# One sort of all 16,384 tokens ahead of the last feed-forward instead of four block sorts, with its rank table and three more row buffers

## The chip, the core and the metric

The kernel runs on one core of a Trainium2 chip. The core has five engines with a queue each, which work on their own and wait for each other by semaphores: TensorE (PE: matrix products and transposes into PSUM), VectorE (DVE), ScalarE (ACT), GpSimd (POOL) and SyncE (SP, which here only starts transfers). Transfers between HBM and the on-chip SBUF run on 16 DMA engines; the indirect ones, which take row numbers from a tile, are started by POOL. Tiles have 128 partitions (rows).

The metric is device time in microseconds (us) of one execution, from the first to the last instruction and what lies around it. Times are medians of several executions. A profile is one execution on its own.

## The reference

Two layers, each a graph convolution and a feed-forward part, over 64 batches of 256 tokens with 256 features. The change lies in the last step, the feed-forward of layer 1, and in how its tokens are ordered:

```python
x = x + _L0_gnn_ref(_layernorm(x), adj, ...)
x = x + _L0_ffn_ref(_layernorm(x), ...)          # a recurrent (LSTM) step over 256 tokens
x = x + _L1_gnn_ref(_layernorm(x), adj, ...)
x = x + _L1_ffn_ref(_layernorm(x), ...)

def _L1_ffn_ref(x, ...):                          # 16,384 tokens, 1024 units
    t = jnp.max(xx[:, None, :] + Wt[None, :, :], axis=-1) + bt
    cvx = jnp.max(z * sl_cvx + of_cvx, axis=-1)   # z = t, 8 lines per unit
    ccv = jnp.min(z * sl_ccv + of_ccv, axis=-1)
    trop = s * cvx + (1.0 - s) * ccv
    classical = gelu(xf @ Wc + bc)
    g = sigmoid(xf @ Wg + bg)
    return (g * trop + (1.0 - g) * classical) @ Wd + bd
```

The costly line is the first: for each token and each of 1024 units a maximum over 256 features of feature plus weight.

## The kernel before

**Stages.** The kernel is one program. The first 2647 us of the profile are the graph step of layer 0, the recurrent step, the preparation of the feed-forward's units, and the graph step of layer 1. That last one (`Batch`, one batch of 256 tokens at a time) also finds, for every token, how many of its 256 features can decide a maximum at all. This number goes to `need`, a tile with one column for each of the 128 groups of 128 tokens. It writes the token's normalised features and a copy with the undecided features masked to `pay_d`, and the residual to `res_d`, both in DRAM.

**Ranks.** The feed-forward (the pools `w4` and following, from L1227) never computes the maximum over 256 features. A token with `need` = 9 only needs its 9 largest features. For tokens with about the same need to share a tile of 128, the tokens are sorted by need, largest first. `RANKS` (L41) says how many features the tiles of a block get, in order: the first tile 40, the second 19, and so on down to 2. If more tokens need many features than the table has room for, a flag is raised (`late`, L243; `over`), and after everything else a dense computation replaces the result (from L1428).

**Blocks.** `RANKS` has 32 entries, so `NB` = 32 tiles (4096 tokens) are sorted together and there are `NSB` = 4 blocks. `sorted_block` (L1247) calls `sort` (L213) for a block and turns the result into row numbers, `perm`. Block 0 is sorted ahead of the loop (L1388); blocks 1 to 3 inside it, each two groups ahead of its first use (L1406).

**What `sort` does.** It is a counting sort on DVE and PE, with `bins` = 41 and `nb` tiles. It makes a one-hot array (bin, tile) of every partition (L221), sums it over the partitions with PE (L236), scans it (L238), adds the places of earlier partitions (L248 and L249), and reduces to a place for each token (L252). It then turns places into an order: `rhot`, a one-hot of the row within a tile (nb × 128 elements, L263), and `thot`, a one-hot of the tile (nb × nb elements, L270, L276, L282), whose nb products on PE (L285) give the token at each place.

**Groups and the loop.** Four tiles of a block make a group (`GT` = 4), chosen so that the ranks of a block's 8 groups come out nearly equal (`mixed`): 47, 36, 36, 35, 35, 35, 34 and 35. Thirty-two groups go through a pipeline (L1392). Iteration g does, four times (once for each tile q):

- `down` of group g−2 (PE, L1218), added to the residual on DVE (L1225), and `give_back`: POOL scatters the result to the output (L1374);
- `ask` of group g+1: POOL gathers 128 token rows from `pay_d` (L1285); `pick`: DVE takes the largest features eight at a time (L1297 to L1300: value, index, removal), PE transposes the features and ACT copies them (L1306);
- `maxplus` of group g: for every rank POOL gathers one row of the weights for each token into a row buffer (L1314, 128 rows of 4 KB), and DVE folds it into `acc` with one instruction (L1323); the first rank of a tile is done by ACT (L1320);
- `classical` of group g−1 (PE, L1338; ACT, L1345) and `fuse`: PE transposes `acc` (L1355), ACT and DVE evaluate the lines (L1200 to L1210, ending in `fu`);
- `ask_rest` of group g−1: POOL gathers the residual rows (L1363).

The row buffers are the pool `row4` with 10 tiles: POOL can start a gather only when the tenth row before it has been used. All gathers and scatters stand in POOL's one queue, in a fixed order.

**What orders the work.** The order on each engine is settled when the program is built: the framework lists every engine's instructions in an order of its own making, near to that of the code, and adds the semaphores. At run time each engine takes its instructions strictly in that order.

Of the kernel before, what the change touches and what calls it, by code (L numbers as in the profile page):

```python
# [11 lines left out]
BF16 = mybir.dt.bfloat16  # L12
# [25 lines left out]
SHIFT = 40.0  # L38
LOW = 2.1
REST = 0.1  # L40
RANKS = [40, 19, 16, 15, 14, 13, 12, 12, 11, 11, 10, 10, 9, 9, 8, 8]  # L41
RANKS += [8, 7, 7, 6, 6, 6, 5, 5, 5, 4, 4, 3, 3, 3, 2, 2]
NEG = -1e30


# [12 lines left out]
def kernel(ctx: ExitStack, tc: tile.TileContext, a: dict, out: bass.AP):  # L58
# [16 lines left out]
    nc = tc.nc  # L75
# [20 lines left out]
    rows = const.tile([P, K], F32, name="rows")  # L96
# [12 lines left out]
    need = const.tile([P, NT], F32, name="need")  # L109
# [13 lines left out]
    num_f = const.tile([P, P], F32, name="num_f")  # L123
# [9 lines left out]

    NB = len(RANKS)
    NSB = NT // NB
# [77 lines left out]
    def sort(sp, psum, need, room, over, tag):  # L213


        nb, bins = need.shape[1], room.shape[1]
        cnt = sp.tile([P, nb], F32, name=f"cnt_{tag}", tag="cnt")
        nc.vector.tensor_scalar(cnt, need, float(bins - 1), None, ALU.min)
        nc.vector.tensor_scalar(cnt, cnt, -1.0, float(bins - 1), ALU.mult, ALU.add)
        hot = sp.tile([P, bins, nb], BF16, name=f"hot_{tag}", tag="hot")  # L220
        nc.vector.tensor_tensor(  # L221
            hot,
            cnt.unsqueeze(1).to_broadcast([P, bins, nb]),
            num_f[:, :bins].unsqueeze(2).to_broadcast([P, bins, nb]),
            ALU.is_equal,
        )
# [11 lines left out]
        nc.vector.tensor_tensor_scan(  # L238
            pos_c, ones[:, 0:1].to_broadcast([P, bins * nb]), tot_c, 0.0, ALU.mult, ALU.add
        )  # L240
        nc.vector.tensor_tensor(pos, pos, tot, ALU.subtract)
# [10 lines left out]
        nc.vector.tensor_reduce(at, pos.rearrange("p k i -> p i k"), AX.X, ALU.add)  # L252
        at_i = sp.tile([P, nb], I32, name=f"ati_{tag}", tag="at_i")
        til = sp.tile([P, nb], F32, name=f"til_{tag}", tag="til")
        row = sp.tile([P, nb], F32, name=f"row_{tag}", tag="row")
        nc.vector.tensor_copy(at_i, at)
        nc.vector.tensor_scalar(at_i, at_i, P - 1, None, ALU.bitwise_and)
        nc.vector.tensor_copy(row, at_i)
        nc.vector.tensor_tensor(til, at, row, ALU.subtract)
        nc.vector.tensor_scalar(til, til, 1.0 / P, None, ALU.mult)  # L260

        rhot = sp.tile([P, nb, P], BF16, name=f"rhot_{tag}", tag="tot")
        nc.vector.tensor_tensor(  # L263
            rhot,
            row.unsqueeze(2).to_broadcast([P, nb, P]),
            num_f.unsqueeze(1).to_broadcast([P, nb, P]),
            ALU.is_equal,
        )
        thot = sp.tile([P, nb, 2, nb], BF16, name=f"thot_{tag}", tag="pos")
        nc.vector.tensor_tensor(  # L270
            thot[:, :, 0, :],
            til.unsqueeze(2).to_broadcast([P, nb, nb]),
            num_f[:, :nb].unsqueeze(1).to_broadcast([P, nb, nb]),
            ALU.is_equal,
        )
        nc.vector.tensor_tensor(  # L276
            thot[:, :, 1, :],
            thot[:, :, 0, :],
            num_f[:, :nb].unsqueeze(2).to_broadcast([P, nb, nb]),
            ALU.mult,  # L280
        )
        nc.vector.tensor_scalar(thot[:, :, 0, :], thot[:, :, 0, :], rows[:, 0:1], None, ALU.mult)  # L282
        pp = psum.tile([P, 2, nb], F32, name=f"pp_{tag}", tag="pc")
        for i in range(nb):
            nc.tensor.matmul(  # L285
                pp, rhot[:, i, :], thot[:, i, :, :], start=(i == 0), stop=(i == nb - 1)
            )
# [57 lines left out]
    with (  # L345
# [18 lines left out]
        class Batch0:  # L364


            def __init__(self, b):
                self.b = b
# [747 lines left out]
    class FeedForward:  # L1116


        def __init__(self, wp, pools, units_sorted):
            self.p4, self.u4, self.cgp, self.ps_c, self.ps_o = pools  # L1120
# [21 lines left out]
            self.s_b = wp.tile([P, NF], F32, name="s_b")  # L1142
            nc.scalar.activation(self.s_a, col["alpha"], AF.Sigmoid)
            nc.vector.tensor_scalar(self.s_b, self.s_a, -1.0, 1.0, ALU.mult, ALU.add)

        def classical(self, xr, tag):

# [76 lines left out]
                    )  # L1224
                nc.vector.tensor_tensor(res[c], res[c], po[:, c, :], ALU.add)  # L1225

    with (  # L1227
        tc.tile_pool(name="w4", bufs=1) as wp,
        tc.tile_pool(name="s4", bufs=1) as sp,
        tc.tile_pool(name="pay4", bufs=5) as payp,  # L1230
        tc.tile_pool(name="xr4", bufs=3) as xrp,
        tc.tile_pool(name="res4", bufs=7) as resp,
        tc.tile_pool(name="tk4", bufs=8) as tkp,
        tc.tile_pool(name="row4", bufs=10) as rowp,
        tc.tile_pool(name="acc4", bufs=8) as accp,
        tc.tile_pool(name="p4", bufs=2) as p4,
        tc.tile_pool(name="u4", bufs=3) as u4,
        tc.tile_pool(name="cg4", bufs=2) as cgp,
        tc.tile_pool(name="fu4", bufs=1) as fup,
        tc.tile_pool(name="ps_c4", bufs=6, space=PSUM) as ps_c,  # L1240
        tc.tile_pool(name="ps_o4", bufs=2, space=PSUM) as ps_o,
    ):
# [4 lines left out]
        def sorted_block(blk):  # L1247


            order = sort(  # L1250
                sp, ps_c, need[:, blk * NB : (blk + 1) * NB], room, over[:, blk : blk + 1], blk
            )
            nc.vector.tensor_copy(perm[blk][:, 0, :], order)
            nc.vector.tensor_scalar(order, order, float(blk * NB * P), None, ALU.add)
            nc.vector.tensor_copy(perm[blk][:, 1, :], order)

        ff = FeedForward(wp, (p4, u4, cgp, ps_c, ps_o), True)

        def place(i, of):
            j = i % NB  # L1260
# [124 lines left out]
            if 0 <= g < NGR:  # L1385
                getattr(groups[g], piece)(*args)

        sorted_block(0)  # L1388
        for q in range(GT):
            groups[0].ask(q)  # L1390
            groups[0].pick(q)
        for g in range(NGR + 2):  # L1392
            for q in range(GT):
                if q == 0:
                    for part in range(GT // NC):
                        each(g - 2, "down", part)
                    each(g - 1, "classical", 0)
                each(g + 1, "ask", q)
                each(g, "maxplus", q)
                each(g - 1, "fuse", q)  # L1400
                if q + 1 < GT:
                    each(g - 1, "classical", q + 1)
                each(g + 1, "pick", q)
                each(g - 1, "ask_rest", q)
                each(g - 2, "give_back", q)
            if g % GPB == GPB - 2 and g + 2 < NGR:  # L1406
                sorted_block((g + 2) // GPB)

# [19 lines left out]
    with tc.If(bad > 0):  # L1428
        with (
# [9 lines left out]
            ff = FeedForward(wp, (p4, u4, cgp, ps_c, ps_o), False)  # L1439
# [123 lines left out]
```

## Time and profile before

| | us |
|---|---|
| time, median of 3 (lowest, highest) | 5418.49 (5399.26, 5419.93) |
| the profiled execution: its time | 5431.3 |
| the profiled execution: its span | 5429.4 |
| sort of block 0 begins, ends | 2646.81, 2674.35 |
| first group's results reach L1225 | 2839.45 |
| last group's results reach L1225 | 5408.23 |

Row gathers (L1314) take 1453.8 us of POOL over 1172 instructions, a mean of 1240 ns; the folding on DVE (L1323) 1317.5 us over 1044, a mean of 1282 ns. The page's table of groups has them as the two costliest lines of the whole kernel.

How to read it: the page gives the busy time of each engine over the whole span, then 40 equal slices of it in tenths, the DMA queues, the chain that ended last, the costliest groups of instructions with the idle time before them and what ended it, and the DMA issues. Where a stage has its own limits, the same trace is asked for the busy time of each engine in a stretch of it, for the list of waits (who waited for whom), and for the instructions in order of time (the timeline; a number in brackets is the idle time before an instruction and what ended it). L1225 is line 1225 of the code before.

### The profile page before, as it was taken

How to read it: one execution, taken by the hardware profiler on the slowest of the kernel's cores; microseconds unless marked ns; L12 is line 12 of the kernel's file. 1: busy time of each engine (PE TensorE's matmuls, PEld its weight loads, DVE VectorE, ACT ScalarE, POOL GpSimd, SP SyncE). 2: the span in 40 equal slices, each digit the busy share in tenths (PEclk: the TensorE clock that was granted, in tenths of full speed). 3: DMA queues.
4: the chain of work that ended last, by engine and by line, in shares of the span. 5: the costliest groups of instructions: out<-in, count | busy, mean ns of one | idle time of the engine just before them, and what ended most of it. 6: DMA issues, size and time to landing. Idle time of an engine off the chain costs nothing. (4 is left out here: it accounts for less than half of the span.)

```text
span 5429.4 us, 58641 instructions
## 1 busy us (share of the span) xinstructions
PE 4221.3 (78%) x17791; PEld 2368.5 (44%) x17792; DVE 4189.6 (77%) x9226; ACT 2273.9 (42%) x4245; POOL 2588.7 (48%) x2739
## 2 busy tenths in 40 slices
PE   8999889999999968888457666677675776757777
PEld 5666533333333346666334443344343443434344
DVE  6777686555555568888788798888898889888897
ACT  3555411222222235555344544455444554445455
POOL 2333400000000035555487667777767777677774
PEclk9999999999999989999678878788787888878889
DMA  4222213111111134444487776877767787777774
GB/s 134 84 82 86 79 21 83 32 28 28 28 28 28 28 108 138 139 139 138 153 304 255 252 254 206 270 252 266 244 224 266 244 272 241 231 260 246 267 253 141
DMA packets 448128, 886.59 MB, mean 163 GB/s; under 512 B 54328, under 2 KB 279100, under 8 KB 447804
## 3 DMA queue, kind: packets, MB, share of 16 engines
q0 software_dynamic: 192448, 685.96, 37.7%
q1 hardware_dynamic: 253476, 193.64, 12.5%
q8 instruction: 143, 2.34, 0.2%
q10 hardware_dynamic: 1880, 3.16, 0.2%
q14 instruction: 181, 1.48, 0.1%
HBM read 773.32 MB, written 110.26 MB: 163 GB/s over the span
## 5 line engine op out<-in xcount | busy, mean ns | idle before, releaser
L1314 POOL DMA_INDIRECT row<-wT_d,num x1172 | 1453.8, 1240 | 547.3 <-issue 271.3
L1323 DVE SCALAR_TENSOR_TENSOR acc<-row,val,acc 128x1024 f32<-128x1024 f32 x1044 | 1317.5, 1282 | 178.2 <-DMA row<-wT_d,num 165.6
L1218 PE MATMUL po<-w_d,fu 128*128 128x256 f32 x2048 | 599.6, 439 | 102.4 <-DVE fu L1210 95.5
L1338 PE MATMUL pc_gg<-xr,w_gt 128*128 128x512 f32 x1024 | 539.9, 669 | 96.0 <-ACT u L1206 60.8
L575 PE MATMUL pg<-w_hh,hT 128*64 128x512 f32 x2040 | 501.5, 613 | 91.4 <-DVE hT L702 91.0
L956 POOL TENSOR_TENSOR adjT<-adjT,ident 128x128 f32<-128x128 f32 x128 | 57.7, 473 | 1020.2 <-DMA adjT<-in_adjT_dram 1012.6
L1218 PEld LDWEIGHTS po<-w_d,fu 128*128 128x128 f32 x2048 | 425.6, 219 | 270.0 <-DVE fu L1210 148.2
L1338 PE MATMUL pc_cl<-xr,w_c 128*128 128x512 f32 x1024 | 490.5, 620 | 20.9 <-issue 11.3
L1206 ACT ACTIVATE u<-pa,prm 128x512 f32<-128x512 f32 x512 | 383.4, 778 | 265.3 <-DVE v L1207 239.0
L575 PE MATMUL pg<-w_ih,XT 128*64 128x512 f32 x2048 | 488.1, 598 | 2.9 <-issue 2.9
L1320 ACT ACTIVATE acc<-row,val 128x1024 f32<-128x1024 f32 x128 | 146.9, 1147 | 762.0 <-DMA row<-wT_d,num 761.8
L682 ACT ACTIVATE sg<-pg 128x256 f32<-128x256 f32 x256 | 98.3, 384 | 839.5 <-PE pg L575 833.3
L1207 DVE SCALAR_TENSOR_TENSOR v<-u,prm,v 128x512 f32<-128x512 f32 x512 | 377.2, 750 | 36.8 <-ACT u L1206 36.0
L1355 PE MATMUL pa<-ident,acc 128*128 128x128 f32 x1024 | 196.6, 327 | 266.4 <-ACT u L1206 91.6
L1338 PEld LDWEIGHTS pc_gg<-xr,w_gt 128*128 128x128 f32 x1024 | 208.8, 213 | 357.7 <-issue 208.6
L173 DVE TENSOR_SCALAR xn<-x,mv,rstd 128x256 f32<-128x256 f32 x512 | 224.9, 454 | 136.5 <-POOL rstd L166 128.5
L1338 PEld LDWEIGHTS pc_cl<-xr,w_c 128*128 128x128 f32 x1024 | 199.6, 201 | 252.5 <-issue 226.7
L1355 PEld LDWEIGHTS pa<-ident,acc 128*128 128x128 f32 x1024 | 146.1, 168 | 341.1 <-ACT u L1206 102.9
L575 PEld LDWEIGHTS pg<-w_ih,XT 128*64 128x64 f32 x2048 | 149.3, 139 | 301.8 <-issue 301.8
L688 DVE TENSOR_TENSOR cc<-sg,cc 128x128 f32<-128x128 f32 x255 | 74.8, 293 | 261.9 <-ACT sg L682 260.6
L1305 PE MATMUL ptx<-ident,pay 128*128 128x128 f32 x256 | 65.6, 346 | 265.5 <-ACT u L1206 123.8
L1200 ACT ACTIVATE v<-pa,prm 128x512 f32<-128x512 f32 x256 | 199.0, 777 | 170.6 <-DVE fu L1210 149.4
(394 smaller groups left out, 8327.0 us busy)
## 6 DMA issues: line engine op xcount, KB each, us to landing
adjT<-in_adjT_dram SPq DMA_DIRECT2D x128, 256.0 KB, 3.3
row<-wT_d,num POOLq DMA_INDIRECT x1172
x<-in_x_dram SPq DMA_DIRECT2D x64, 256.0 KB, 2.7
x_d<-x SPq DMA_DIRECT2D x64, 256.0 KB, 2.5
x1s<-x_d SPq DMA_DIRECT2D x128, 128.0 KB, 2.9
x_d<-x1s SPq DMA_DIRECT2D x128, 128.0 KB, 2.5
x<-x_d SPq DMA_DIRECT2D x64, 256.0 KB, 2.8
res_d<-x SPq DMA_DIRECT2D x64, 256.0 KB, 3.8
```

Of the source, the lines that this page charges most:

```text
L173: nc.vector.tensor_scalar(xn[:, c, :], x[:, c, :], mv[:, c, 0:1], rstd[:, c : c + 1], ALU.subtract, ALU.mult)
L575: ins = nc.tensor.matmul(half(pg, j), by(k), gates_of(w, k, j), start=False, stop=(last and k == K - 1), tile_position=(0, j * B),)
L682: nc.scalar.activation(sg, pg[:, : 2 * P], AF.Sigmoid)
L1200: nc.scalar.activation(v, pa, AF.Identity, bias=prm[:, f, 1:2], scale=prm[:, f, 0:1])
L1206: nc.scalar.activation(u, pa, AF.Relu, bias=of, scale=sc)
L1207: nc.vector.scalar_tensor_tensor(v, u, sg, v, ALU.mult, ALU.add)
L1218: nc.tensor.matmul(po[:, c, :], fused(f, c), self.w_d[:, f, :], start=False, stop=(f == NF - 1),)
L1314: nc.gpsimd.indirect_dma_start(row, None, wT_d, bass.IndirectOffsetOnAxis(ap=self.num[q][:, r : r + 1], axis=0))
L1320: nc.scalar.activation(acc, row, AF.Identity, bias=v)
L1323: nc.vector.scalar_tensor_tensor(acc, row, v, acc, ALU.add, ALU.max)
L1338: nc.tensor.matmul(pc, wgt[:, k, f * P : (f + 1) * P], self.xr[:, k, :], start=(k == 0), stop=(k == K - 1),)
L1355: nc.tensor.transpose(pa[:, q * P : (q + 1) * P], self.acc[q][:, f * P : (f + 1) * P], ident)
```

## The change

The rank table has 128 entries instead of 32, so that the same code makes one block of 128 tiles: `NB` = 128, `NSB` = 1. Its entries sum to 1065; four times the old table is 1172. The groups become 32 of one block, with 43, 35, 35, 34, 33 and then 32 to 34 ranks. `pay_d`, `res_d` and `perm` become one tensor each. There is one call of `sort` with 5248 elements in its (bin, tile) arrays, and it stands ahead of the loop in pools of its own, which are closed before the loop's pools are opened. The two calls of `sorted_block` go. In `sort` the one-hots are made in chunks of 16 tiles with two alternating buffers, and the scaling of `thot` by the row number moves from DVE to ACT. The row buffers go from 10 to 13. `FeedForward` gets its pools by a method of its own (`use`), since it is now built before they are.

```diff
-RANKS = [40, 19, 16, 15, 14, 13, 12, 12, 11, 11, 10, 10, 9, 9, 8, 8]
-RANKS += [8, 7, 7, 6, 6, 6, 5, 5, 5, 4, 4, 3, 3, 3, 2, 2]
+RANK_COUNTS = (
+    (40, 1), (24, 1), (21, 1), (19, 1), (18, 1), (17, 2), (16, 3), (15, 3), (14, 4), (13, 5),
+    (12, 6), (11, 7), (10, 9), (9, 9), (8, 11), (7, 11), (6, 11), (5, 11), (4, 11), (3, 9), (2, 7),
+    (1, 4),
+)
+RANKS = [rank for rank, count in RANK_COUNTS for _ in range(count)]
...
-        rhot = sp.tile([P, nb, P], BF16, name=f"rhot_{tag}", tag="tot")
...
-        nc.vector.tensor_scalar(thot[:, :, 0, :], thot[:, :, 0, :], rows[:, 0:1], None, ALU.mult)
         pp = psum.tile([P, 2, nb], F32, name=f"pp_{tag}", tag="pc")
...
+        ch = min(nb, 16)
+        for i0 in range(0, nb, ch):
+            some = slice(i0, i0 + ch)
+            rhot = sp.tile([P, ch, P], BF16, name=f"rhot_{tag}_{i0}", tag=f"rhot{i0 // ch % 2}")
+            nc.vector.tensor_tensor(
+                rhot,
+                row[:, some].unsqueeze(2).to_broadcast([P, ch, P]),
+                num_f.unsqueeze(1).to_broadcast([P, ch, P]),
+                ALU.is_equal,
+            )
+            thot = sp.tile([P, ch, 2, nb], BF16, name=f"thot_{tag}_{i0}", tag=f"thot{i0 // ch % 2}")
+            nc.vector.tensor_tensor(thot[:, :, 0, :], ..., ALU.is_equal)
+            nc.vector.tensor_tensor(thot[:, :, 1, :], ..., ALU.mult)
+            nc.scalar.activation(thot[:, :, 0, :], thot[:, :, 0, :], AF.Copy, scale=rows[:, 0:1])
+            for i in range(ch):
+                nc.tensor.matmul(
+                    pp,
+                    rhot[:, i, :],
+                    thot[:, i, :, :],
+                    start=(i0 + i == 0),
+                    stop=(i0 + i == nb - 1),
+                )
...
-        tc.tile_pool(name="s4", bufs=1) as sp,
...
-        tc.tile_pool(name="row4", bufs=10) as rowp,
...
+        with (
+            tc.tile_pool(name="s4", bufs=1) as sp,
+            tc.tile_pool(name="ps_s4", bufs=2, space=PSUM) as ps_s,
+        ):
+            for blk in range(NSB):
+                order = sort(
+                    sp, ps_s, need[:, blk * NB : (blk + 1) * NB], room, over[:, blk : blk + 1], blk
+                )
+                nc.vector.tensor_copy(perm[blk][:, 0, :], order)
+                nc.vector.tensor_scalar(order, order, float(blk * NB * P), None, ALU.add)
+                nc.vector.tensor_copy(perm[blk][:, 1, :], order)
...
+        rowp = ctx4.enter_context(tc.tile_pool(name="row4", bufs=13))
...
-        sorted_block(0)
         for q in range(GT):
             groups[0].ask(q)
...
-            if g % GPB == GPB - 2 and g + 2 < NGR:
-                sorted_block((g + 2) // GPB)
```

More of the change, by code (lines that the diff above doesn't have):

```diff
@@ L260, in sort @@
         nc.vector.tensor_scalar(til, til, 1.0 / P, None, ALU.mult)
-        rhot = sp.tile([P, nb, P], BF16, name=f"rhot_{tag}", tag="tot")
[L263 to L281, printed above, removed]
-        nc.vector.tensor_scalar(thot[:, :, 0, :], thot[:, :, 0, :], rows[:, 0:1], None, ALU.mult)
-        pp = psum.tile([P, 2, nb], F32, name=f"pp_{tag}", tag="pc")
-        for i in range(nb):
-            nc.tensor.matmul(
-                pp, rhot[:, i, :], thot[:, i, :, :], start=(i == 0), stop=(i == nb - 1)
-            )
+        pp = psum.tile([P, 2, nb], F32, name=f"pp_{tag}", tag="pc")
@@ new lines, in sort @@
+        ch = min(nb, 16)
[7 more added lines that the diff above has]
+                ALU.is_equal,
+            )
+            thot = sp.tile([P, ch, 2, nb], BF16, name=f"thot_{tag}_{i0}", tag=f"thot{i0 // ch % 2}")
+            nc.vector.tensor_tensor(
+                thot[:, :, 0, :],
+                til[:, some].unsqueeze(2).to_broadcast([P, ch, nb]),
+                num_f[:, :nb].unsqueeze(1).to_broadcast([P, ch, nb]),
+                ALU.is_equal,
+            )
+            nc.vector.tensor_tensor(
+                thot[:, :, 1, :],
+                thot[:, :, 0, :],
+                num_f[:, some].unsqueeze(2).to_broadcast([P, ch, nb]),
+                ALU.mult,
+            )
[8 more added lines that the diff above has]
+                )
@@ L1116, with __init__ @@
     class FeedForward:
-        def __init__(self, wp, pools, units_sorted):
-            self.p4, self.u4, self.cgp, self.ps_c, self.ps_o = pools
+        def __init__(self, wp, units_sorted):
             self.w_c = wp.tile([P, K, FF], F32, name="w_c")
@@ L1144, in __init__, with use @@
             nc.vector.tensor_scalar(self.s_b, self.s_a, -1.0, 1.0, ALU.mult, ALU.add)
+        def use(self, p4, u4, cgp, ps_c, ps_o):
+            self.p4, self.u4, self.cgp, self.ps_c, self.ps_o = p4, u4, cgp, ps_c, ps_o
         def classical(self, xr, tag):
@@ L1225, in down @@
                 nc.vector.tensor_tensor(res[c], res[c], po[:, c, :], ALU.add)
-    with (
-        tc.tile_pool(name="w4", bufs=1) as wp,
-        tc.tile_pool(name="s4", bufs=1) as sp,
[L1230 to L1233, printed above, removed]
-        tc.tile_pool(name="row4", bufs=10) as rowp,
[L1235 to L1242, printed above, removed]
+    with ExitStack() as ctx4:
+        wp = ctx4.enter_context(tc.tile_pool(name="w4", bufs=1))
         room = room_of(wp, RANKS)
@@ L1245 @@
         over = wp.tile([P, NSB], F32, name="over")
[L1247 to L1257, printed above, removed]
+        ff = FeedForward(wp, True)
+        with (
[5 more added lines that the diff above has]
+                    sp, ps_s, need[:, blk * NB : (blk + 1) * NB], room, over[:, blk : blk + 1], blk
+                )
+                nc.vector.tensor_copy(perm[blk][:, 0, :], order)
+                nc.vector.tensor_scalar(order, order, float(blk * NB * P), None, ALU.add)
+                nc.vector.tensor_copy(perm[blk][:, 1, :], order)
+        payp = ctx4.enter_context(tc.tile_pool(name="pay4", bufs=5))
+        xrp = ctx4.enter_context(tc.tile_pool(name="xr4", bufs=3))
+        resp = ctx4.enter_context(tc.tile_pool(name="res4", bufs=7))
+        tkp = ctx4.enter_context(tc.tile_pool(name="tk4", bufs=8))
+        rowp = ctx4.enter_context(tc.tile_pool(name="row4", bufs=13))
+        accp = ctx4.enter_context(tc.tile_pool(name="acc4", bufs=8))
+        p4 = ctx4.enter_context(tc.tile_pool(name="p4", bufs=2))
+        u4 = ctx4.enter_context(tc.tile_pool(name="u4", bufs=3))
+        cgp = ctx4.enter_context(tc.tile_pool(name="cg4", bufs=2))
+        fup = ctx4.enter_context(tc.tile_pool(name="fu4", bufs=1))
+        ps_c = ctx4.enter_context(tc.tile_pool(name="ps_c4", bufs=6, space=PSUM))
+        ps_o = ctx4.enter_context(tc.tile_pool(name="ps_o4", bufs=2, space=PSUM))
+        ff.use(p4, u4, cgp, ps_c, ps_o)
         def place(i, of):
@@ L1438 @@
         ):
-            ff = FeedForward(wp, (p4, u4, cgp, ps_c, ps_o), False)
+            ff = FeedForward(wp, False)
+            ff.use(p4, u4, cgp, ps_c, ps_o)
             w_t = wp.tile([P, NF, D], F32, name="w_trop")
```

## The prediction

> **What bounds the kernel now.** First the page's busy shares and slices. The sort and the feed-forward are the last 2782 us of the span (from 2646.8), and VectorE (DVE) is the fullest engine there.
>
> ```profile
> PE 4221.3 (78%) x17791; PEld 2368.5 (44%) x17792; DVE 4189.6 (77%) x9226; ACT 2273.9 (42%) x4245; POOL 2588.7 (48%) x2739
> ...
> DVE  6777686555555568888788798888898889888897
> ```
>
> Then the busy time by stretch. Columns: stretch, its length, busy us (and instructions) of PE, weight loads, DVE, ACT, POOL, then granted clock, DMA share, GB/s.
>
> ```profile
> 2646.80:2674.70 27.90, 6.06 (x41) 3.69 (x42) 24.60 (x34) 0.00 (x0) 0.01 (x1) 0.50 0.23 85
> 2674.70:2839.45 164.75, 75.42 (x192) 35.84 (x192) 138.27 (x192) 59.78 (x79) 132.46 (x107) 0.68 0.87 300
> 3537.93:3619.14 81.21, 55.54 (x169) 30.81 (x170) 70.71 (x98) 41.57 (x56) 59.16 (x49) 0.86 0.73 245
> 3174.87:3245.50 70.63, 46.88 (x135) 27.34 (x136) 68.08 (x99) 28.37 (x40) 51.00 (x38) 0.77 0.70 228
> 3245.50:3358.57 113.07, 76.89 (x249) 42.74 (x248) 92.09 (x135) 45.40 (x64) 75.78 (x54) 0.79 0.61 202
> 3358.57:3455.75 97.18, 55.29 (x161) 31.77 (x160) 83.50 (x110) 42.29 (x55) 72.71 (x57) 0.72 0.83 273
> 2839.45:5375.64 2536.19, 1763.02 (x5385) 999.64 (x5386) 2188.09 (x3044) 1212.51 (x1624) 1827.72 (x1441) 0.83 0.75 249
> ```
>
> The first row is the first block's sort: DVE alone, the others wait. The second is the fill, before the first group comes out. From 2839.45 on I cut the time where DVE does the first L1225 of each group; 30 rounds up to 5375.64. Nineteen of them (the third row is one) average 82.7 us with about 70 of DVE. Three times in the run three rounds (rows four to six: 280.9 us; the other two triples 269.7 and 271.4) hold a block's sort and its 47-rank group; the last two rounds are short (69.9 and 72.1). Over the 30 rounds DVE idles 2536 − 2188 = 348 us. The waits of DVE and of POOL in that stretch name the causes:
>
> ```profile
> DVE acc L1323 <- DMA row<-wT_d,num: 147.9, 41, 10.3
> DVE res L1225 <- remote: 62.1, 14, 6.3
> ...
> POOL row L1314 <- ACT acc L1320: 150.7, 65, 5.2
> ```
>
> (us, times, longest.) DVE starves for gathered rows 148 us in all, and hands over to `down` some 8 us a round (6.1 + 1.1 + 0.8 in the timeline). POOL meanwhile waits 151 us for ACT, and 48 for DVE, to give a row buffer back. So DVE bounds the loop, with POOL just behind: a round issues some 47 indirect DMAs, and by the rows
>
> ```profile
> L1314 POOL DMA_INDIRECT row<-wT_d,num x1083 | 1341.6, 1239 | 520.2 <-issue 251.2 <-ACT acc L1320 150.7 <-DVE acc L1323 47.9
> L1323 DVE SCALAR_TENSOR_TENSOR acc<-row,val,acc 128x1024 f32<-128x1024 f32 x969 | 1221.5, 1282 | 157.8 <-DMA row<-wT_d,num 147.9 <-ACT xr L1306 5.6 <-PE ptx L1305 2.2
> ```
>
> that is 47 × (1.24 + 0.30 between two) = 72 us of POOL.
>
> **The sort, +88 us.** One sort of 128 tiles replaces the first one (2646.81 to 2674.35: 27.5 us). It stands where DVE alone works, so all of it is on the path; POOL's first asks wait for `perm`, and PE, ACT and the DMA queues wait for those. Rows of the first sort:
>
> ```profile
> 2651.25 2.89 DVE L238 TENSOR_TENSOR_SCAN pos<-ones,tot 128x1312 f32<-128x1312 f32 x1
> 2654.17 1.52 DVE L241 TENSOR_TENSOR pos<-pos,tot 128x1312 f32<-128x1312 f32 x1
> ...
> 2659.34 2.34 DVE L252 TENSOR_REDUCE at<-pos 128x32 f32<-128x1312 f32 x1
> ...
> 2663.78 4.42 DVE L263 TENSOR_TENSOR rhot<-row,num_f 128x4096 bf16<-128x4096 f32 x1
> ```
>
> 1312 elements take 1.52 us and 4096 take 4.42: 1.04 ns an element and 0.16 fixed. The (bin, tile) arrays grow to 41 × 128 = 5248 elements: three such ops (L221, L241, L250) 5.6 each, 16.8; the scan 11.1; the reduce 8.9; the eleven copies and eleven adds at the pitch of the first sort (0.60 for 512) 12.4. One-hots: eight chunks of three ops of 2048, 24 × 2.29 = 55. Some twenty small ops 4. Sum 108. The scaling goes to ACT: 128x1024 takes 1.15 and 128x512 0.69 there, so 2.1 for 2048; PE does 16 products a chunk. Both lie under the 6.9 us that DVE spends on the next chunk, save behind the last: 2.1 + 3.4 + 2 of hand-over. So 115.5, less 27.5: +88. If each chunk waited for ACT and PE (two chunk buffers), 8 × 5.5 more: +132; if nothing waited and the broadcasts ran like the cheapest row, +75.
>
> **Sorts and 47-rank groups inside the loop, −77 us.** The nine rounds of the triples take 822.0, nine plain ones 744.7. The three later sorts, and the 11 or 12 ranks by which those groups exceed the others, go. By busy time it is three times about 34 us (243.7 in the triple shown, against 3 × 70), so up to −102; at least −60 if the lull in the first round of each was itself a gain.
>
> **Ranks elsewhere, −85 us.** The tables sum to 4 × 293 = 1172 before and 1065 after. Leaving out the groups with 47 and the fill, 35.1 a round become 32.9: 2.24 × 30 = 67 ranks. Each is a gather on POOL (1.54) and an op on DVE, which follow at 1.2 us; I take DVE's 1.2, being the fullest: 81, and 4 for four groups with one pick round fewer (three ops of a third of a us). Ends: 0.76 × 1.2 (in the triples 34 us of DVE work cost 26) gives 61, POOL's 1.54 gives 103. The fill has five ranks fewer at the 1.6 us of its pace: −8.
>
> **13 row buffers, −70 us.** No row of before has three more buffers. The ends are −148, all of DVE's wait for rows, and +18: three more rows in the queue may hold up `pay`, for which L1297 waits 18.4 us now, as long again. In the programs as built, when POOL comes to a group's first write-out it has issued 10 rows more than DVE used by then, and 13 after; the numbers of rows between write-outs stay. In the round of 3537.93 DVE then runs dry for 6.6 us, behind POOL's 15 us of write-outs and reads of `res` and `pay`. Three more rows with what lies between them are about 4.5 us of DVE work. Cutting 4.2 off each plain round's idle time beyond 8 gives 2.9 a round, 87 in 30; I take 2.3, since POOL (45 DMAs, 70 us) has little slack.
>
> The smaller sort at 811 us only moves one 0.23 us op to ACT, inside the recurrent stage: nothing; uncovered, 1 us. The 41 fills of `room` and the weight loads stay ahead of the sort.
>
> **Sum.** +88 − 77 − 85 − 8 − 70 = −152. The profiled execution took 5431.3 (span 5429.4): 5279. It lies 12.8 above the median of three, 5418.5; on that base 5266.
>
> **Rivals.** *Buffers change nothing*, because the dry spell is POOL's stretch of small DMAs: 5266 + 70 = 5336. For it: DMA share falls to 0.2 to 0.4 in that stretch and is near 1.0 behind it. Against: the stock at its start is what grows.
>
> *POOL becomes the bound*, as its issues stretch beside a denser DVE: at the 1.5 us of many gathers, 45 × 1.80 = 81 us a round, loop 30 × 81 − 24 = 2406, so −130 + 88 − 8 = −50: 5368. Against it, POOL beside eight back-to-back L1323:
>
> ```profile
> 3605.11 0.94 POOL L1314 DMA_INDIRECT row<-wT_d,num  x1 [0.31 <-issue]
> 3606.36 0.94 POOL L1314 DMA_INDIRECT row<-wT_d,num  x1 [0.30 <-issue]
> ```
>
> The Trainium skill, "SBUF — State Buffer", section "Who interferes with whom", says that a VectorE op with two SBUF inputs contends with a GpSimd instruction that reads SBUF, one holding the other off; L1323 is such an op. By that rule this rival would hold; the trace agrees only in part, with 0.94 beside many of them.
>
> *Slower: the loop is not DVE's*, but the chain of hand-overs (DVE's last `fu`, PE's `down`, L1225; ACT's `u`, DVE's `v`). Then sorts and ranks come out of idle time, and only the sort's +88 and the fill's −8 stay: 5498. It decides once the 206 us of DVE work taken out (three sorts of 22, 107 ranks of 1.2, 12 of picks) give back under 80. For it: 8 us of hand-over in each round. Against: 70 of 82.7 us busy, and extra work in the triples that cost three quarters of itself.
>
> *It doesn't do what it says*: more tokens need many ranks than the new table has, a bin is late (L243), and the dense path at the end runs: 8 × 256 × 8 DVE ops of 128x2048, 2.35 us each by the rows of 512 and 1024, 38 ms. Counted from the reference's inputs, each count of the table holds with at least 99 tokens to spare.
>
> **How the numbers follow.** As summed, 5215 to 5315: 0.58. Buffers change nothing: 0.17. POOL's bound: 0.10. Better than 5215 (POOL's price for ranks, all row waits gone): 0.08. Slower: 0.06. Dense path: 0.01. The range 5195 to 5365 leaves out the last two and half of the two ahead of them, 0.16. About 0.5%, 27 us, is what a measurement can tell: faster 0.91, same 0.03, slower 0.06.
>
> **What would show it.** Sort: about 115 us of DVE alone ahead of the first ask. Rounds: no more triples, 76 to 78 us each with DVE about 67 busy; 937 L1323 ops. Buffers: DVE's wait for rows near 80 us or below, POOL's for buffers lower. I am wrong if rounds stay at 81 and over, or if DVE waits within the sort between chunks.

## The result, and the profile after

The changed kernel takes 5246.13 us (median of four runs, 5222.39 to 5250.29), the kernel before 5408.88 (four runs, 5391.71 to 5419.93) beside it. The ratio is 0.9692, with a 95% interval of 0.9656 to 0.9728: 163 us less by the medians. The profiled execution took 5222.39, 24 below its median, and the one of before, 5431.3, lay 22 above the 5408.88. So the two profiles differ by 209 us (spans 5429.4 and 5220.5), and the terms read from them add up to that, not to 163.

First the page of the changed kernel: busy time of each engine, and the slices of VectorE.

```profile
PE 4202.8 (81%) x17789; PEld 2335.0 (45%) x17790; DVE 4065.2 (78%) x9017; ACT 2275.0 (44%) x4248; POOL 2424.4 (46%) x2632
...
DVE  6777776555555557888878887888888998999896
```

DVE does 124 us less in all. Then the changed kernel by stretch, with the columns of the table shown for before (busy us of PE, weight loads, DVE, ACT, POOL; granted clock, DMA share, GB/s):

```profile
2647.97:2769.60 121.63, 39.36 (x153) 20.73 (x154) 107.08 (x69) 16.01 (x8) 0.00 (x0) 0.55 0.00 0
2769.60:2923.80 154.20, 71.99 (x194) 34.77 (x195) 132.07 (x187) 60.30 (x80) 122.26 (x103) 0.71 0.89 307
3398.10:3470.85 72.75, 55.51 (x177) 31.83 (x176) 64.37 (x89) 39.68 (x55) 57.41 (x44) 0.88 0.77 255
3928.52:4002.22 73.70, 58.46 (x177) 32.63 (x176) 66.54 (x97) 39.96 (x55) 55.93 (x45) 0.86 0.78 259
2923.80:5166.43 2242.63, 1719.24 (x5271) 954.07 (x5269) 1989.29 (x2807) 1196.72 (x1617) 1673.90 (x1338) 0.88 0.77 258
```

The rows are the sort, the fill, two plain rounds, and all 30 rounds. (L1238 is now the line that was L1225, the add to `res`, by which the rounds are cut; L1339 is the fold L1323, L1330 the gather L1314, L1336 ScalarE's first rank L1320, L1219 and L1220 `u` and `v`.) The sort takes 121.6 us instead of 27.5 (+94), the fill 154.2 instead of 165.1 (−11), the 30 rounds 2242.6 instead of 2536.2 (−294), and what lies around them +2: −209. The triples are gone; the first 28 rounds average 74.9 us. DVE idles 2242.6 − 1989.3 = 253 us in the rounds, where it idled 348.

The sort in the timeline (start, duration, engine, line, operation, idle time before it):

```profile
2662.55 11.09 DVE L242 TENSOR_TENSOR_SCAN pos<-ones,tot 128x5248 f32<-128x5248 f32 x1
2673.68 5.62 DVE L245 TENSOR_TENSOR pos<-pos,tot 128x5248 f32<-128x5248 f32 x1
...
2692.61 8.91 DVE L256 TENSOR_REDUCE at<-pos 128x128 f32<-128x5248 f32 x1
...
2719.52 2.29 DVE L271 TENSOR_TENSOR rhot<-row,num_f 128x2048 bf16<-128x2048 f32 x1 [3.54 <-PE pp L292]
...
2734.19 2.29 DVE L271 TENSOR_TENSOR rhot<-row,num_f 128x2048 bf16<-128x2048 f32 x1 [1.25 <-PE pp L292]
...
2748.86 2.29 DVE L271 TENSOR_TENSOR rhot<-row,num_f 128x2048 bf16<-128x2048 f32 x1 [1.25 <-PE pp L292]
...
2768.20 0.29 DVE L300 TENSOR_SCALAR order<-pp 128x128 f32<-128x128 f32 x1 [5.78 <-PE pp L292]
```

The single operations cost what was forecast of them. DVE does wait between chunks, three times, for PE to have read an older chunk's buffer: 3.54 + 1.25 + 1.25 = 6.0 us in all; and 5.8 behind the last chunk.

The page's groups that answer to those of before:

```profile
L1330 POOL DMA_INDIRECT row<-wT_d,num x1065 | 1288.0, 1209 | 444.2 <-issue 235.4
L1339 DVE SCALAR_TENSOR_TENSOR acc<-row,val,acc 128x1024 f32<-128x1024 f32 x937 | 1175.8, 1275 | 23.2 <-DMA row<-wT_d,num 21.9
...
L1220 DVE SCALAR_TENSOR_TENSOR v<-u,prm,v 128x512 f32<-128x512 f32 x512 | 373.1, 745 | 187.4 <-ACT u L1219 186.9
...
L1336 ACT ACTIVATE acc<-row,val 128x1024 f32<-128x1024 f32 x128 | 147.3, 1151 | 652.4 <-DMA row<-wT_d,num 652.0
```

And the waits of DVE and POOL between 2755 and 5200 us (us, times, longest):

```profile
DVE v L1220 <- ACT u L1219: 186.9, 49, 9.8
DVE res L1238 <- PE po L1231: 55.5, 44, 5.8
DVE acc L1339 <- DMA row<-wT_d,num: 21.9, 15, 5.9
...
POOL row L1330 <- ACT acc L1336: 102.2, 63, 5.0
```

The same stretch of the kernel before:

```profile
DVE acc L1323 <- DMA row<-wT_d,num: 146.0, 44, 10.3
DVE res L1225 <- remote: 56.0, 13, 6.3
DVE res L1225 <- PE po L1218: 41.1, 32, 4.7
DVE v L1207 <- ACT u L1206: 34.1, 11, 8.9
...
POOL row L1314 <- ACT acc L1320: 140.1, 59, 5.2
POOL row L1314 <- DVE acc L1323: 40.7, 55, 3.3
```

DVE's waits for rows are nearly gone: 21.9 us, where before has 146.0. But its waits for ScalarE's `u` rose from 34.1 to 186.9. That was not forecast. Over the 30 rounds alone DVE's idle time goes from 348 to 253 us as follows: rows 146 to 10, the waits at `res` (the result of `down`) 128 to 54, the waits of `v` 34 to 188, all else 40 to 1. The timeline of the round from 3928.52 shows how it comes about:

```profile
3965.44 1.15 ACT L1336 ACTIVATE acc<-row,val 128x1024 f32<-128x1024 f32 x1 [11.84 <-DMA row<-wT_d,num]
3966.50 0.76 ACT L1219 ACTIVATE u<-pa,prm 128x512 f32<-128x512 f32 x1
3966.86 0.94 POOL L1330 DMA_INDIRECT row<-wT_d,num  x1 [2.00 <-ACT acc L1336]
3967.29 0.75 DVE L1220 SCALAR_TENSOR_TENSOR v<-u,prm,v 128x512 f32<-128x512 f32 x1 [6.96 <-ACT u L1219]
```

ScalarE works in order. Its next instruction was the first rank of a tile, whose row came late, behind a stretch in which POOL issued only write-outs and reads of `res`. ScalarE stood 11.84 us; the `u` behind it in its queue ran at once when it was done, and DVE stood 6.96 us for it. Laid beside ScalarE's timeline, DVE's 49 waits for `u` show ScalarE standing at a first rank for 95 of the 187 us and working on one for 39; most of the rest is `u` itself (41). POOL, too, waited 2.00 us for ScalarE to give the buffer back. What was a wait of DVE for a row has in part become a wait of ScalarE for a row and of DVE for ScalarE.

### The profile page after: what moved, and what is told of

It reads as the page before. It is cut to its first block, busy times and chain, and to the rows that moved or that the text cites. A ratio compares the mean times of both kernels' runs of the same rounds, so it can differ in the third digit from the quotient of the medians.

```text
span 5220.5 us, 58067 instructions
## 1 busy us (share of the span) xinstructions
PE 4202.8 (81%) x17789; PEld 2335.0 (45%) x17790; DVE 4065.2 (78%) x9017; ACT 2275.0 (44%) x4248; POOL 2424.4 (46%) x2632
## 5 line engine op out<-in xcount | busy, mean ns | idle before, releaser
L1330 POOL DMA_INDIRECT row<-wT_d,num x1065 | 1288.0, 1209 | 444.2 <-issue 235.4
L1339 DVE SCALAR_TENSOR_TENSOR acc<-row,val,acc 128x1024 f32<-128x1024 f32 x937 | 1175.8, 1275 | 23.2 <-DMA row<-wT_d,num 21.9
L1354 PE MATMUL pc_cl<-xr,w_c 128*128 128x512 f32 x1024 | 518.8, 647 | 162.2 <-ACT u L1219 142.1
L1231 PE MATMUL po<-w_d,fu 128*128 128x256 f32 x2048 | 553.7, 413 | 78.9 <-DVE fu L1223 77.9
L1220 DVE SCALAR_TENSOR_TENSOR v<-u,prm,v 128x512 f32<-128x512 f32 x512 | 373.1, 745 | 187.4 <-ACT u L1219 186.9
L1231 PEld LDWEIGHTS po<-w_d,fu 128*128 128x128 f32 x2048 | 395.4, 204 | 227.0 <-DVE fu L1223 136.4
L1336 ACT ACTIVATE acc<-row,val 128x1024 f32<-128x1024 f32 x128 | 147.3, 1151 | 652.4 <-DMA row<-wT_d,num 652.0
L1219 ACT ACTIVATE u<-pa,prm 128x512 f32<-128x512 f32 x512 | 382.6, 777 | 102.9 <-DVE v L1220 102.1
L1371 PE MATMUL pa<-ident,acc 128*128 128x128 f32 x1024 | 184.6, 308 | 152.6 <-ACT u L1219 57.9
L586 PEld LDWEIGHTS pg<-w_hh,hT 128*64 128x64 f32 x2040 | 125.0, 137 | 288.9 <-issue 148.1
```

What stands on the lines that cost most here:

```text
L586: ins = nc.tensor.matmul(half(pg, j), by(k), gates_of(w, k, j), start=False, stop=(last and k == K - 1), tile_position=(0, j * B),)
L1219: nc.scalar.activation(u, pa, AF.Relu, bias=of, scale=sc)
L1220: nc.vector.scalar_tensor_tensor(v, u, sg, v, ALU.mult, ALU.add)
L1231: nc.tensor.matmul(po[:, c, :], fused(f, c), self.w_d[:, f, :], start=False, stop=(f == NF - 1),)
L1330: nc.gpsimd.indirect_dma_start(row, None, wT_d, bass.IndirectOffsetOnAxis(ap=self.num[q][:, r : r + 1], axis=0))
L1336: nc.scalar.activation(acc, row, AF.Identity, bias=v)
```

## The experiments

Ratios are to the kernel before, run beside each on the same chip, with their 95% intervals. A hundredth of a ratio is 54 us.

**Ten row buffers on the changed kernel.**

```diff
-        rowp = ctx4.enter_context(tc.tile_pool(name="row4", bufs=13))
+        rowp = ctx4.enter_context(tc.tile_pool(name="row4", bufs=10))
```

> The changed kernel with 10 row buffers in place of 13; all else as changed. My theory: the three buffers carry VectorE over GpSimd's stretch of small transfers and are worth about 70 us, so 5246 + 70 = 5316 (0.983 of the kernel before), with VectorE's wait for rows back at 100 to 150 us. Rival: the row waits fell because there are fewer ranks, and the buffers do nothing: 5246 within 15 us, 0.970, VectorE's row wait still near 20 us.

Measured: 5302.31 us, 0.9812 (0.9783 to 0.9840), 56 us above the changed kernel's median, 65 by the ratios. DVE's waits in this kernel:

```profile
DVE v L1220 <- ACT u L1219: 136.7, 28, 9.5
DVE acc L1339 <- DMA row<-wT_d,num: 95.3, 44, 7.3
DVE res L1238 <- PE po L1231: 83.5, 43, 5.8
```

From ten buffers to 13, the waits for rows fall by 73 us and those for `po` by 28, and those for `u` rise by 50: 51 us net. This stretch ends some 70 us before the loop with ten buffers does; over the whole of both profiles it is 80, 30 and 46, so 64 net, and the two executions are 68 apart. The buffers act on the rows as forecast, and ScalarE gives part of it back.

**Sixteen row buffers.** (`bufs=13` becomes 16.)

> The changed kernel with 16 row buffers. My theory: in the changed kernel late rows no longer stop VectorE itself but ScalarE, which waits at the first rank of a tile with the lines for VectorE queued behind it (VectorE waits 187 us for ScalarE's u); three more buffers cut that wait by a third to two thirds, so 5246 - 60 to - 120: 5126 to 5186 (0.948 to 0.959). Rival: ScalarE's u is late for another reason (TensorE, table loads) or GpSimd's issue is now the bound: no gain, 5246 within 15 us (0.970), the wait for u still above 150 us.

Measured: 5207.06 us, 0.9637 (0.9609 to 0.9665), 39 us below the changed kernel's median (30 by the ratios); the intervals overlap. Its waits:

```profile
DVE v L1220 <- ACT u L1219: 169.0, 44, 14.2
...
DVE acc L1339 <- DMA row<-wT_d,num: 18.8, 13, 5.8
```

The wait for `u` was expected to fall by a third to two thirds; it fell by a tenth, and the gain is smaller than forecast. This profile is 21 us shorter than that of the changed kernel, and 20 of them lie in the 30 rounds, where the waits of `v` are 21 us less, those for rows 6 less and those at `res` 4 more. The changed kernel's profile was its fastest run, which is why the medians are further apart.

**The old counts in one block.** One sort of 128 tiles, but each entry of the old table four times, 1,172 ranks in place of 1,065.

```diff
+RANKS = [rank for rank in RANKS for _ in range(4)]
```

> The changed kernel with the old rank table, each entry four times: one sort of 128 tiles and 13 buffers as changed, but 1172 ranks instead of 1065. My theory: a rank costs what VectorE takes for it, 1.2 us, so 107 ranks and ten pick rounds more are 128 + 10: 5384 (0.995). By GpSimd's price of 1.54 us it is 165 more, 5411 (1.000). Rival: the loop hangs on the hand-overs between engines and ranks come out of idle time: at most 40 more, 5286 (0.977).

Measured: 5381.64 us, 0.9952 (0.9933 to 0.9970): 0.0260 more than the changed kernel, 141 us (136 by the medians), for 107 ranks and ten rounds of picks. The expected time held. That is 1.3 us a rank, close to the 1.2 at which VectorE's folds follow one another.

**Four sorts of 32 tiles ahead of the loop**, with the old table in the changed kernel; 13 row buffers.

```diff
-RANK_COUNTS = (
...
-RANKS = [rank for rank, count in RANK_COUNTS for _ in range(count)]
+RANKS = [40, 19, 16, 15, 14, 13, 12, 12, 11, 11, 10, 10, 9, 9, 8, 8]
+RANKS += [8, 7, 7, 6, 6, 6, 5, 5, 5, 4, 4, 3, 3, 3, 2, 2]
```

> The changed kernel with the old table of 32 entries: four block sorts, all ahead of the loop, 1172 ranks, the eight groups of each block with 47 to 34 ranks, 13 buffers. My theory: four sorts of 27.5 us take 110 where the one of 128 tiles takes 122, so this is the wide table less 12: 5372 (0.993), VectorE alone for about 110 us ahead of the first gather. Rival: sorts that stand in the loop cost nothing there, and the groups with 47 ranks were the dear part of the triples: then this run is 25 us or more slower than the wide table, 5410 or more.

Measured: 5377.66 us, 0.9937 (0.9913 to 0.9960). The old counts in four blocks and in one cannot be told apart (0.9937 and 0.9952): it is the number of ranks that pays, not how the sort is cut. This time, too, was the one expected, though not by its terms: by the timeline the four sorts take 97.8 us, not 110, which is 24 less than the one sort, and the 30 rounds with their 47-rank groups take 31 more (2407 against 2376).

**The same with ten row buffers.**

> The kernel with the four sorts of before put ahead of the loop and the old table (1,280 ranks), with ten row buffers in place of 13. What is open is how the 31 us between before and the run with four sorts ahead are shared. Theory one (a buffer is worth as much here as on the changed kernel, because the sorts no longer stand in the loop): 56 us more than with 13 buffers, about 5434, so the sorts ahead alone cost some 25 us. Rival (with 1,280 ranks more rows in flight are worth nothing, as the kernel before with 12 buffers showed): within 10 us of 5378, so the sorts ahead alone bring the 31.

(The old table has 4 × 293 = 1,172 ranks, not 1,280.) Measured: 5408.34 us, 1.0019 (1.0006 to 1.0032). Against 13 buffers that is 0.82%, 44 us, nearer to theory one (56) than to the rival (none). So the sorts ahead alone cost 10 us (3 to 17 by the interval), and the buffers bring 44. Two neighbouring rounds of this kernel by stretch:

```profile
3322.91:3402.42 79.51, 58.02 (x176) 31.20 (x176) 71.73 (x108) 40.02 (x56) 58.59 (x50) 0.89 0.80 273
3402.42:3496.13 93.71, 54.56 (x161) 32.49 (x161) 83.61 (x109) 43.25 (x56) 73.25 (x56) 0.72 0.81 275
```

The second holds a group of 47 ranks: 12 us more of DVE and 14 of time. Without a sort there is no triple left, only this one long round.

**Twelve row buffers on the kernel before.**

```diff
-        tc.tile_pool(name="row4", bufs=10) as rowp,
+        tc.tile_pool(name="row4", bufs=12) as rowp,
```

> The kernel before with 12 row buffers in place of 10, and nothing else (13 don't fit beside its sort's tiles). My theory: buffers help by themselves, since the stretch of small transfers is in every round; three of them were worth 56 us on the changed kernel, two should bring 35 to 55 on the kernel before: 5356 to 5376 (0.990 to 0.9935). Rival: they only help once the loop has fewer ranks and no sorts: no gain, 1.000 within 0.003.

Measured: 5408.52 us, 0.9993 (0.9979 to 1.0007): no gain; what I expected failed. Its waits tell why:

```profile
DVE v L1207 <- ACT u L1206: 119.4, 19, 13.2
DVE acc L1323 <- DMA row<-wT_d,num: 83.9, 34, 8.6
```

The waits for rows fell by 62 us (from 146.0) and those at `res` by 36 (119 to 83), those for `u` rose by 85 (from 34.1). Here the trade that costs the changed kernel a part of its gain ate all of it but some 13 us, and the time shows none.

**POOL multiplies in the sort.** One of the three one-hot operations of a chunk goes to POOL, with four chunk buffers instead of two, so that nothing waits for a buffer.

```diff
-            nc.vector.tensor_tensor(
+            nc.gpsimd.tensor_tensor(
                 thot[:, :, 1, :], ..., ALU.mult)
```

> The changed kernel with the second one-hot product of each chunk (eight ops of 2048) on GpSimd instead of VectorE, and four chunk buffers instead of two. Theory one: VectorE loses 8 x 2.2 us and its waits between chunks, GpSimd does them in some 5 us each (128x512 takes 1.26 us there) beside it, 40 us against VectorE's 36, so the sort falls from 122 to about 110: 5234 (0.968). Rival, by the port rule of the Trainium skill (an op of VectorE with two inputs in SBUF and a GpSimd op that reads SBUF hold each other off): the two run one after the other, 36 + 40 us where it was 55, so 20 us longer: 5266 (0.973).

Measured: 5241.48 us, 0.9698 (0.9673 to 0.9723), not to be told from the changed kernel. The sort takes 124.2 us by this kernel's timeline, 2.6 more. Theory one had asked for some 110, the rival for 20 more. DVE has eight operations of 2.28 us fewer and yet wins nothing:

```profile
2729.34 2.28 DVE L271 TENSOR_TENSOR rhot<-row,num_f 128x2048 bf16<-128x2048 f32 x1
...
2729.49 5.59 POOL L284 TENSOR_TENSOR thot<-thot,num_f 128x2048 bf16<-128x2048 bf16 x1 [2.23 <-DVE thot L278]
2731.54 5.69 DVE L278 TENSOR_TENSOR thot<-til,num_f 128x2048 bf16<-128x2048 f32 x1
...
2768.63 3.61 POOL L284 TENSOR_TENSOR thot<-thot,num_f 128x2048 bf16<-128x2048 bf16 x1 [2.29 <-DVE thot L278]
```

The last product, beside which DVE does nothing, takes POOL 3.61 us; the others take 5.5 to 5.6, two more, as long as DVE's L271 lasts when they come. DVE's next operation takes 5.69 in place of 2.28: it lasts until POOL is done, and then its own time more. Each holds the other off. The sum comes out: eight operations fewer are −18.3 us and the waits for a buffer −6.0, but seven operations of DVE take 3.4 longer each, +23.9, and the wait behind the last chunk grows from 5.8 to 8.9. So the rival's mechanism was right, and its price too high. The Trainium skill, "SBUF — State Buffer", section "Who interferes with whom", calls the port pair that these two engines share an exclusive lock, for which a VectorE operation with two SBUF inputs contends with a GpSimd instruction that reads SBUF; for two element-wise operations this trace agrees, 5.69 against 2.28.

**The first rank on VectorE**, on the changed kernel.

```diff
-                        nc.scalar.activation(acc, row, AF.Identity, bias=v)
+                        nc.vector.tensor_scalar(acc, row, v, None, ALU.add)
```

> The changed kernel with the first rank of each tile (a row plus a scalar, 128 instructions) on VectorE instead of ScalarE. My theory: VectorE's wait of 187 us for ScalarE's u is ScalarE standing at that instruction for a late row, with u behind it. Then that wait falls under 60 us, VectorE waits for rows itself again (60 to 130 us instead of 22), and it has 128 x 0.6 to 1.2 us more to do: 5246 to 5320 in all (0.970 to 0.984). Rival: u is late because of TensorE or of the table loads: the wait for u stays above 140 us, and the time grows by the whole 77 to 154 us, 5323 to 5400.

Measured: 5174.81 us, 0.9576 (0.9554 to 0.9598): 71 us below the changed kernel (63 by the ratios) and below the range expected, though DVE has more to do. From its page:

```profile
L1330 POOL DMA_INDIRECT row<-wT_d,num x1065 | 1323.3, 1243 | 356.1 <-issue 262.6
...
L1220 DVE SCALAR_TENSOR_TENSOR v<-u,prm,v 128x512 f32<-128x512 f32 x512 | 373.4, 748 | 4.6 <-ACT u L1219 1.9
```

and from its waits:

```profile
DVE res L1238 <- PE po L1231: 53.8, 45, 4.7
DVE acc L1336 <- DMA row<-wT_d,num: 40.1, 11, 12.1
```

The wait for `u` is 1.9 us where it was 186.9. In return DVE does 128 operations of 0.742 us (median of L1336, now on DVE) and waits 40.1 + 8.6 us for rows in place of 21.9. Over the 30 rounds its idle time falls from 253 to 124 us (`v` 188 to 0, `res` 54 to 76, rows 10 to 44) and its busy time grows from 1989 to 2068; the rounds get 51 us shorter and the profile 58. It was expected to be no gain because a late row would stop DVE in ScalarE's place; it does so 11 times.

**The same line on the kernel before**, with ten row buffers and with 12.

> The kernel before with one line changed: the first rank of a tile, acc = row + val, on VectorE (0.742 us in the run with the first rank on VectorE) instead of ScalarE (1.15 us); ten row buffers as before. Theory one (ScalarE stands in its order at a late first row, and u, which VectorE needs, stands behind it): before has only 34 us of VectorE's waits for u to give, against 128 x 0.742 = 95 us of new VectorE work, of which its 143 us of waits for rows may take a part; so between 5377 (all of it absorbed) and 5472, middle 5425. Rival (taking 128 x 1.15 us off ScalarE is a gain by itself, whatever the buffers): as large a gain as on the changed kernel, 5411 - 71 = 5340.

> The kernel before with the same line changed and 12 row buffers in place of ten. With 12 buffers alone the waits for rows fell from 143 to 78 us and those for u rose from 34 to 119, and the time stood still. Theory one (the row that ScalarE stands at turned the one wait into the other): with the first rank on VectorE the wait for u cannot come back, so 12 buffers are worth 40 to 70 us against ten with the same line, 5365 to 5385. Rival (the loop of before has no use for more rows in flight, since POOL or the transfers set the rate at which rows come): within 10 us of the run with ten buffers and the same line.

Measured: 5321.97 us, 0.9853 (0.9827 to 0.9879), and 5306.97 us, 0.9837 (0.9818 to 0.9855), both beside 5395.51. Theory one failed on both. With ten buffers the gain is 74 us, as large as on the changed kernel, which is what the rival of that run had said, and the two further buffers bring nothing that can be told apart. The waits with ten buffers:

```profile
DVE acc L1320 <- DMA row<-wT_d,num: 70.0, 13, 9.2
DVE res L1225 <- PE po L1218: 59.8, 63, 3.1
...
DVE acc L1323 <- DMA row<-wT_d,num: 10.7, 12, 3.8
```

I had counted only the 34 us for `u` as ScalarE's. But the waits for rows also fall, from 146.0 to 70.0 + 10.7, with no buffer added, and POOL's waits for a buffer back from 140.1 + 40.7 to 76.9 + 38.7. ScalarE, standing in its order, gave row buffers back late, POOL gathered late, and DVE's waits for rows were in part ScalarE's doing. The waits at `res` fall as much, from 119 to 60: TensorE stood behind ScalarE too, 261 us for `u` before and 53 now.

One rival to this reading was not tried. A program with the first rank on VectorE is listed anew by the framework, and not only the moved operations stand elsewhere: by operation and tile, about 2,360 of VectorE's 2,822 others from 2700 us on keep the order that they have in the changed kernel, and on the kernel before some 2,440 of 2,976. What the new order is worth by itself no run shows.

**Sixteen and ten row buffers with the first rank on VectorE**, on the changed kernel.

> The changed kernel with the first rank on VectorE and 16 row buffers in place of 13. With the first rank on VectorE and 13 buffers 48 us of VectorE's waits for rows are left in the loop, those for u are 2, and 54 for the down projection. Theory one: at most those 48 us can come out, and 16 buffers were worth 39 on the changed kernel with the first rank on ScalarE: 5135 to 5165, and the best of all these kernels. Rival (VectorE, 2068 of 2192 us busy in the rounds, is all that is left): 5175, no change.

> The changed kernel with the first rank on VectorE and ten row buffers in place of 13. From 13 to ten cost 56 us with the first rank on ScalarE. Theory one (buffers set when rows land; a late row now stops VectorE itself, not ScalarE and then VectorE): still a cost, seen in VectorE's own waits for rows, 5205 to 5235. Rival (the buffers acted only by way of ScalarE's order): within 15 us of 5175.

Measured: 5157.55 us, 0.9549 (0.9535 to 0.9564) with 16, and 5180.58 us, 0.9599 (0.9580 to 0.9618) with ten. The first is the fastest of all these kernels, 238 us below the kernel before beside it. Its time is within what theory one expected, but not for its reason, which was that waits for rows would come out. They did not:

```profile
DVE acc L1336 <- DMA row<-wT_d,num: 40.7, 15, 6.5
DVE acc L1339 <- DMA row<-wT_d,num: 16.5, 12, 4.7
```

That is 57 us, where 13 buffers have 49; the 15 us by the ratios (17 by the medians) are not explained, and the intervals just overlap. With ten buffers the kernel is 0.23% slower than with 13, some 12 us (6 by the medians) and inside the intervals, where it was 1.2% with the first rank on ScalarE: here the rival of that run held. With ten buffers, DVE's waits for rows:

```profile
DVE acc L1336 <- DMA row<-wT_d,num: 80.8, 23, 10.5
...
DVE acc L1339 <- DMA row<-wT_d,num: 5.0, 9, 1.0
```

That is 37 us more than with 13, of which the time shows a third. The kernels with ten, 13 and 16 buffers and the first rank on VectorE have the same order of operations on VectorE, ScalarE and TensorE, so they differ in nothing but buffers and POOL's queue. Most of what the three buffers brought in this change was cover for ScalarE's place in the chain.

## Why the prediction was right

The time forecast was 5266, measured 5246, on a base of 5418 there and 5409 here; the change forecast was −152, measured −163. The mechanism held, two terms were mis-sized, by 29 and 26 us, and it was luck that their errors went against each other. The runs split the change into four steps, each as a difference of ratios times 5409 us:

| step | ratio before and after it | us |
|---|---|---|
| sorts ahead of the loop, ten buffers | 1.0000 to 1.0019 | +10 |
| 13 row buffers | 1.0019 to 0.9937 | −44 |
| one block with the old counts | 0.9937 to 0.9952 | +8 (not resolved) |
| the finer table, 107 ranks fewer | 0.9952 to 0.9692 | −141 |
| all | | −167 |

*The sort, +88.* Right: +94 in the trace. The sum of the operations held. I had written that DVE waiting between chunks would prove me wrong; it did wait, 6.0 us, the size of the miss and far from the 44 of the bound.

*Sorts and 47-rank groups, −77.* Mis-sized, and at its bound of −102. Ahead of the loop the four sorts take 97.8 us, the three later ones 70 of them, and moving them there cost 10 net, so the loop gained some 60 by them alone. The 35 ranks by which three groups exceeded the others, at 1.3 us, are 46 more: −106. (One block in place of four adds 24 us of sort and only 8 of time, so the loop gained a little more by it; the intervals leave that open.) The triples, held against as many plain rounds, did not show all of the cost: the 25 plain rounds with four sorts ahead and ten buffers average 80.6 us, where before had 82.7, though their ranks and buffers are the same. How much of these 2 us is the sorts', and how much the high profile of before, is not settled.

*Ranks elsewhere, −85, and the fill, −8.* Right: the remaining 72 ranks, the fill's five among them, are 94 at 1.3 us; the 11 that the fill gave are part of that.

*13 row buffers, −70.* Right in sign and in the rows, too large: 44 us with the old ranks, 56 to 65 with the new. The step that failed is that I let the row waits simply go. I had said what was late next in a plain round (the hand-overs), but not that ScalarE stands at a first row with `u` behind it. Its price for the hand-overs was also that of one round: 8 us in the round shown, while the waits at `res` of all 30 rounds are 128 us, 4.3 a round.

*Rounds.* Forecast 76 to 78 us with DVE about 67 busy, no triples, 937 folds; measured 74.9 with 66.6 and 937, in a profile that lay 24 us below its median, 0.8 a round.

*The rivals.* That the buffers change nothing is ruled out by the pairs with ten and 13. POOL did not become the bound: it waits 102 + 40 us for buffers to come back, and the gathers got no dearer beside a denser DVE (1209 ns, before 1240). They do pay for DVE, though, and did so before: in the changed kernel all 120 gathers in whose first 0.9 us DVE ran nothing (101) or only operations with one SBUF input (19) took 0.97 us or less, and the 906 that had an operation with two SBUF inputs beside them for at least half of that time took 1.255 on average (before: 119 of 122, and 999 with 1.284). The rule of the Trainium skill, "SBUF — State Buffer", section "Who interferes with whom", fits these gathers as it fits POOL's multiply, if issuing one counts as an instruction that reads SBUF. The price stood in both kernels, and POOL had room for it. The slower case, a loop that hangs on hand-overs, was closer than its chance says: the wait for `u` is of that kind and grew by 153 us, but the waits at `res`, of that kind too, fell by 64 and those for rows by 124, and the ranks that went came out of the time in full. The dense path did not run.

## What to carry to other kernels

An engine that works in order and stands at late data makes everything behind it late, so read which instructions stand behind a wait, not only how long the wait is; an engine busy 44% of the time can cost the busiest one 187 us. A deeper buffer moves a wait before it removes it: look for the wait that grew. Where a small operation binds an engine to an irregular transfer, try it on the engine that consumes the data anyway; here 85 us more busy time on the busiest engine went with a kernel 71 us faster.

## What the runs showed of the hardware

VectorE's and POOL's element-wise operations on SBUF held each other off entirely (5.69 us for one of 2.28 beside one of 3.61), while beside VectorE's operations with two SBUF inputs POOL's gathers alone paid: 1.255 us on average in place of 0.94, and the folds took 1.275 with POOL busy beside them and 1.268 without. The add of a per-partition number over 128x1024 took 0.742 us on VectorE and 1.151 on ScalarE. The granted TensorE clock was 0.891 over before's span, 0.912 over the changed kernel's and 0.922 with the first rank on VectorE; what decides it was not tried.
